# A windowed-attention block, rebuilt on full tiles: two score groups per transpose, values on both partition halves, key blocks made on ScalarE, three row buffers

## The chip, the cores and the metric

One core of a Trainium2 chip runs the whole program. The metric is device time in microseconds (us) of one execution. Three engines matter here: TensorE (PE in the profile; the loading of its stationary operand is shown apart, as PEld), VectorE (DVE) and ScalarE (ACT). GpSimd (POOL) and SyncE (SP) issue transfers and do small work. Each engine takes its instructions strictly in the order of its own queue; that order was fixed when the program was built, by a scheduler that interleaves everything the program contains.

## The reference, cut to what matters

Sixteen images of 56 x 56 positions and 128 channels go through four layers, each with its own group normalisation and a residual. Only the first layer, windowed attention, is touched by the change.

```python
def _L0_conv_ref(x, w_qkv, pos_emb, w_out, b_out):   # x: (16, 56, 56, 128)
    x = jnp.roll(x, (-DISP, -DISP), axis=(1, 2))      # DISP = 3
    q, k, v = jnp.split(x @ w_qkv, 3, axis=-1)
    q, k, v = (to_windows(q), to_windows(k), to_windows(v))  # 8 x 8 windows of 7 x 7, 4 heads of 32
    dots = jnp.einsum('bhwid,bhwjd->bhwij', q, k) * scale
    dots = dots + bias[None, None, None] + MASK[None, None]
    attn = jax.nn.softmax(dots, axis=-1)
    out = jnp.einsum('bhwij,bhwjd->bhwid', attn, v)
...
    return jnp.roll(out @ w_out + b_out, (DISP, DISP), axis=(1, 2))
...
x = x + _L0_conv_ref(_gn(x), ...)   # windowed attention
x = x + _L1_conv_ref(_gn(x), ...)   # triangle product
x = x + _L2_conv_ref(_gn(x), ...)   # Fourier attention
x = x + _L3_conv_ref(_gn(x), ...)   # bilinear
```

## The kernel before

Everything is fp32. An image lies in on-chip memory as `xt`, 128 channels on the partitions and 3136 positions along them. Images run in two lanes: even images in lane 0, odd ones in lane 1, each with its own working area (`arena`), its own two one-bank PSUM buffers (`psb`) and its own two-bank PSUM buffer (`psd`). Every image passes the four blocks in turn; the two lanes run beside each other, so the program is eight pairs of images, and within a pair both lanes are in the same block most of the time, lane A (the first to start) a little ahead of lane B.

The attention block (`_window_attention`, `run` from line 526) takes an image in eight rows of eight windows. A window has 49 positions, a row 392. For each row, in the order of the code:

- lines 544 to 546 gather the normalised row into `xw` (DVE does the part of seven windows, POOL the wrapped eighth); `xw` and all that follows lie in one of two halves of the arena, chosen by the row's parity;
- lines 547 to 549: queries on PE (408 columns), copied with a scale to `qt` by ACT;
- lines 550 to 559: keys on PE, then eight small copies (32 partitions x 196), four on DVE (line 559) and four on ACT (line 557), that place each head's 32 channels of the keys into `kblks`, two block tiles that are zero elsewhere (cleared once, line 530). With them one matmul scores all four heads of a window: the other heads' channels meet zeros. There is one such pair of tiles for all rows;
- lines 560 to 565: values, eight matmuls in two PSUM buffers of 49 partitions x 512, each copied to `vt` by ACT;
- lines 568 to 585: scores, two banks of four windows; even windows on partitions 0 to 63, odd ones on 64 to 127; DVE adds the bias on the way to `st`, 784 wide, in 16 groups (four pairs of windows x four heads) of 49;
- lines 586 to 594: the softmax over those 16 groups, five DVE instructions and one exponential on ACT (line 591);
- lines 596 to 603: 16 transposes of 128 x 49, four to a PSUM buffer; each of the four 49 x 512 results is copied to `atn`, two by DVE and two by ACT;
- lines 604 to 615: 32 small matmuls (49 x 32 stationary, 49 columns) weigh the values; ACT copies the result to `ot`;
- lines 616 to 620: the output projection, which DVE adds into `xt` in three pieces (six in the last row).

A row asks for 12 `psb` buffers in turn, and its lane has two, so each third request waits until the first buffer has been read out. In fp32 a matmul is issued as two passes on PE; a transpose is one.

Of the kernel before, what the change touches and what calls it, by code (L numbers as in the profile page):

```python
# [37 lines left out]
AF = mybir.ActivationFunctionType  # L38
# [4 lines left out]
P = 128  # L43
# [8 lines left out]
WS, DISP, NW = 7, 3, 8  # L52
WIN = WS * WS
NH0 = 4
ROWC = NW * WIN
# [38 lines left out]
def _constants():  # L94

    c = {}
# [29 lines left out]
    c["heads"] = np.kron(np.eye(8), np.ones((16, 1)))  # L126

    w, j, l33 = np.arange(P), np.arange(T), np.arange(33)
# [15 lines left out]
    C, S = cs(range(T))  # L144
    both("dv", (C, -S), (S, C))
    C, S = cs([e[1] for e in ENT])
    both("dx", (C, -S), (S, C))
    C, S = cs([e[2] for e in ENT])
    both("dya", (C, -S), (S, C))
    both("dyb", (-S, -C), (C, -S))  # L150
    C, S = cs([e[2] for e in MIR])
    both("dmx", (C, -S), (S, C))
    C, S = cs([e[3] for e in MIR])
# [4 lines left out]
    C, S = (pad(z) for z in cs([_rho(r, 14) for r in range(28)]))  # L158
# [20 lines left out]
    a = 2 * np.pi * np.outer(j, j) / T  # L179
    C, S = np.cos(a), np.sin(a)  # L180
# [4 lines left out]
    a = 2 * np.pi * np.outer(np.arange(32), w) / P  # L185
# [304 lines left out]
def _window_attention(env):  # L490
    e = _Env(env)
# [34 lines left out]
    def run(b, xt):  # L526
        nm, rs = e.group_norm(xt, W("bout0"))
        ar = e.arena()
        half_arena = 5120
        nc.gpsimd.memset(ar[:, 2 * half_arena : 2 * half_arena + 1568], 0.0)  # L530
        kblks = [
            ar[:, o : o + 784].rearrange("p (w h j) -> p w h j", w=NW // 2, h=NH0)
            for o in (2 * half_arena, 2 * half_arena + 784)
        ]
        for k in range(2):
            nc.gpsimd.memset(ar[:, k * half_arena + ROWC : k * half_arena + 408], 0.0)
        for wi in range(NW):
            o = wi % 2 * half_arena
            xw, qt, vt, st, atn, ot = (
                ar[:, o + a : o + a + n]  # L540
                for a, n in ((0, 408), (408, 408), (816, 1024), (1840, 784), (2624, 2048), (4672, ROWC))
# [5 lines left out]
            p = e.psb()  # L547
            mm(p[:, :408], lhsT=W("wqkv")[:, 0:128], rhs=xw, start=True, stop=True)
            nc.scalar.mul(qt, p[:, :408], scale)
            p = e.psb()  # L550
            mm(p[:, :ROWC], lhsT=W("wqkv")[:, 128:256], rhs=row, start=True, stop=True)
            for k, kb in enumerate(kblks):
                for h in range(NH0):
                    s = slice(32 * h, 32 * h + 32)
                    src = p[s, 196 * k : 196 * k + 196].rearrange("p (w j) -> p w j", j=WIN)
                    if h % 2:
                        nc.scalar.copy(kb[s, :, h, :], src)
                    else:
                        nc.vector.tensor_copy(kb[s, :, h, :], src)
            for g in range(2):  # L560
                p = e.psb()
                for i in range(4):
                    w = 4 * g + i
                    mm(p[:WIN, i * P : (i + 1) * P], lhsT=row[:, w * WIN : (w + 1) * WIN], rhs=W("wqkv")[:, 256:384], start=True, stop=True)
                nc.scalar.copy(vt[:WIN, g * 512 : (g + 1) * 512], p[:WIN, :])

            var = 1 if wi == NW - 1 else 0
            for bank in range(2):
                sc = e.psb()
                for w in range(4 * bank, 4 * bank + 4):  # L570
                    col = (w // 2 % 2) * 196
                    half = (w % 2) * 64
                    mm(
                        sc[half : half + 64, col : col + 196],
                        lhsT=qt[:, w * WIN : w * WIN + 64],
                        rhs=kblks[bank][:, w % 4].rearrange("p h j -> p (h j)"),
                        start=True,
                        stop=True,
                    )
                tt(  # L580
                    st[:, bank * 392 : bank * 392 + 392].rearrange("p (a h j) -> p a h j", a=2, h=NH0),
                    sc[:, :392].rearrange("p (a h j) -> p a h j", a=2, h=NH0),
                    bc(bias[:, var, 2 * bank : 2 * bank + 2, :], 2, NH0),
                    ALU.add,
                )
            s3 = st.rearrange("p (a j) -> p a j", j=WIN)
# [4 lines left out]
            act(st, st, AF.Exp)  # L591
# [4 lines left out]
            for g in range(4):  # L596
                p = e.psb()
                for i in range(4):
                    nc.tensor.transpose(p[:WIN, i * P : (i + 1) * P], s3[:, 4 * g + i, :], C("ident"))
                if g % 2:  # L600
                    nc.scalar.copy(atn[:WIN, g * 512 : (g + 1) * 512], p[:WIN, :])
                else:
                    nc.vector.tensor_copy(atn[:WIN, g * 512 : (g + 1) * 512], p[:WIN, :])
            p = e.psb()
            for w in range(NW):
                for h in range(NH0):
                    c0 = (w // 2 * NH0 + h) * P + (w % 2) * 64
                    mm(
                        p[32 * h : 32 * h + 32, w * WIN : (w + 1) * WIN],
                        lhsT=vt[:WIN, w * P + 32 * h : w * P + 32 * h + 32],  # L610
                        rhs=atn[:WIN, c0 : c0 + WIN],
                        start=True,
                        stop=True,
                    )
            nc.scalar.copy(ot, p[:, :ROWC])
# [895 lines left out]
```

## Time and profile before

| what | value |
|---|---|
| median of 8 runs | 13180.7 us (13156.99 to 13234.26) |
| the profiled execution | 13178.56 us, of which the instructions' span is 13176.8 us |
| mean granted TensorE clock | 0.865 of full speed |
| instructions in the span | 201901 |
| first matmul of line 608 in each pair | at 83, 1710, 3307, 4965, 6594, 8222, 9892 and 11539 us |
| attention in the second pair | first gather at 1674 us, last addition into `xt` at 1917 us |

The profile is one execution taken by the hardware profiler. Busy time is counted by engine; matmuls are pipelined, so the end of each is modelled, and a busy PE is not PE at its peak. A line such as L608 is a line of the kernel's source. A count of matmuls counts passes, so 32 matmuls show as 64. PEclk is the share of TensorE's clock that was granted.

### The profile page before, as it was taken

The numbers are of one execution on the slowest core, as the hardware profiler recorded it, in microseconds if no ns is written. First come the engines' busy times: TensorE is split into PE (matmuls) and PEld (weight loads), VectorE is DVE, ScalarE is ACT, GpSimd is POOL, SyncE is SP. The second block draws the span as 40 slices with busy tenths as digits, with TensorE's granted clock in tenths as the row PEclk, the third lists the DMA queues.
The fourth block names the chain that finished last, engine by engine and source line by source line (L and its number), as shares of the span: only waits on it lengthen the run. The fifth ranks groups of instructions, "written<-read, shape, count | busy, mean of one in ns | idle before, by whom it ended". The sixth has DMA issues, their size and how long they took to land. (4 is left out here: it accounts for less than half of the span.)

```text
span 13176.8 us, 201901 instructions
## 1 busy us (share of the span) xinstructions
PE 10162.4 (77%) x82624; PEld 5597.4 (42%) x82624; DVE 9352.2 (71%) x12225; ACT 3777.2 (29%) x6598; POOL 2474.3 (19%) x3387
## 2 busy tenths in 40 slices
PE   7787688876878768787688876878768787687876
PEld 4444255432545325453254532545325453254532
DVE  7775777768676576875768757676576765767757
ACT  4223142231413314232141321413214132141321
POOL 0132101330012300123002230022300223002230
PEclk9887898988988889888898888988889888898887
DMA  1265913569045690346904478044690446904468
GB/s 35 58 183 182 333 40 87 154 212 336 8 99 142 222 325 9 109 132 237 313 5 122 119 260 294 1 124 117 235 314 6 112 129 237 313 6 112 129 240 304
DMA packets 1091754, 2105.90 MB, mean 160 GB/s; under 512 B 98320, under 2 KB 974096, under 8 KB 1089680
## 3 DMA queue, kind: packets, MB, share of 16 engines
q1 hardware_dynamic: 560000, 823.95, 18.9%
q0 software_dynamic: 165120, 629.61, 17.8%
q10 hardware_dynamic: 365712, 639.44, 13.3%
q8 instruction: 654, 10.72, 0.3%
q14 instruction: 268, 2.20, 0.1%
HBM read 1412.73 MB, written 667.03 MB: 158 GB/s over the span
## 5 line engine op out<-in xcount | busy, mean ns | idle before, releaser
L1426 DVE TENSOR_TENSOR arena<-arena 128x1792 f32<-128x1792 f32 x1344 | 2645.2, 2017 | 639.6 <-PE psb L371 313.3
L1213 DVE TENSOR_TENSOR arena<-arena 112x1344 f32<-112x1344 f32 x1024 | 1565.4, 1553 | 364.7 <-DMA arena<-table 347.6
L371 PE MATMUL psb<-arena,cst 128*32 128x448 f32 x9792 | 1526.7, 657 | 0.0
L1211 POOL DMA_DIRECT2D arena<-table x2048 | 1057.3, 518 | 1977.8 <-DMA arena<-table 491.4
L368 PE MATMUL psb<-arena,cst 128*32 128x448 f32 x1408 | 798.1, 654 | 805.7 <-DVE arena L1426 768.4
L371 PE MATMUL psb<-arena 128*64 128x448 f32 (+2 forms) x4864 | 1256.9, 534 | 0.0
L368 PE MATMUL psb<-arena 112*64 112x448 f32 (+1 forms) x1280 | 693.4, 627 | 361.7 <-DVE arena L1103 220.5
L416 POOL TENSOR_TENSOR arena<-arena,power 112x32 f32<-112x32 f32 x224 | 839.4, 3765 | 106.1 <-DVE arena L1357 101.1
L371 PE MATMUL psd<-arena 112*64 112x224 f32 (+1 forms) x3072 | 770.4, 476 | 0.0
L368 PE MATMUL psd<-arena 112*64 112x448 f32 x1024 | 568.9, 642 | 177.8 <-DVE arena L1213 161.7
L371 PEld LDWEIGHTS psb<-arena 112*64 112x64 f32 (+1 forms) x4864 | 451.9, 155 | 523.4 <-issue 516.1
L1411 ACT COPY arena<-psd 128x896 f32<-128x896 f32 x336 | 303.6, 905 | 1251.9 <-DVE arena L1426 682.1
L368 PEld LDWEIGHTS psb<-arena,cst 128*32 128x32 f32 x1408 | 122.5, 120 | 1243.7 <-DVE arena L1426 961.2
L1103 DVE TENSOR_TENSOR arena<-w,coef 128x1792 f32<-128x1792 f32 x256 | 507.8, 2018 | 111.5 <-PE psb L371 91.3
L371 PE MATMUL psd<-arena,wgt 128*32 128x448 f32 x2688 | 533.6, 625 | 39.9 <-DMA arena<-padded 39.3
L371 PEld LDWEIGHTS psb<-arena,cst 128*32 128x32 f32 x9792 | 363.0, 124 | 447.2 <-issue 427.7
L688 PE MATMUL psd<-wgt,arena 128*64 128x128 f32 x7168 | 489.5, 282 | 45.1 <-DVE arena L700 34.5
L368 PE MATMUL psd<-arena,wgt 128*32 128x448 f32 x896 | 452.5, 626 | 81.6 <-DMA arena<-padded 59.8
L688 PEld LDWEIGHTS psd<-wgt,arena 128*64 128x64 f32 x7168 | 422.0, 138 | 177.6 <-issue 126.6
L917 PE MATMUL psb<-cst,arena 128*128 128x64 f32 (+1 forms) x2688 | 431.0, 330 | 67.9 <-ACT arena L884 35.1
L1325 ACT COPY w<-psb 128x448 f32<-128x448 f32 x336 | 178.5, 531 | 1017.9 <-PE psb L371 646.0
L917 PEld LDWEIGHTS psb<-cst,arena 128*128 128x128 f32 x2688 | 419.4, 245 | 107.9 <-ACT arena L884 40.0
(302 smaller groups left out, 19327.7 us busy)
## 6 DMA issues: line engine op xcount, KB each, us to landing
arena<-table POOLq DMA_DIRECT2D x2048, 294.0 KB, 9.1
dy<-w ACTq DMA_DIRECT2D x336, 1792.0 KB
arena<-dy SPq DMA_DIRECT2D x1344, 448.0 KB
arena<-padded SPq DMA_DIRECT2D x896, 162.8 KB
w<-x SPq DMA_DIRECT2D x112, 224.0 KB
out<-w SPq DMA_DIRECT2D x112, 224.0 KB
padded<-w ACTq DMA_DIRECT2D x336, 62.0 KB
arena<-arena POOLq DMA_DIRECT2D x16, 784.0 KB, 9.0
```

Of the source, the lines that this page charges most:

```text
L368: done = mm(**first)
L371: mm(**kw)
L416: ptt(dst, src, w, ALU.pow)
L688: mm(p[half : half + 64, i // 4, i % 4 * P : (i % 4 + 1) * P], lhsT=xh[:, c0 : c0 + 64], rhs=W(w).rearrange("p (k c) -> p k c", c=64)[:, : ...
L917: mm(p[:, 2 * i * nl : 2 * (i + 1) * nl], lhsT=src[:, t * P : (t + 1) * P], rhs=fc, start=True, stop=True)
L1103: tt(t4, bc(ys[c][:, l0 : l0 + 4, :], 1, 8), bc(coef[:, c, h0 : h0 + 8, l0 : l0 + 4], 3, T), ALU.mult,)
L1211: nc.gpsimd.dma_start(out=t[hh * T : (hh + 1) * T, :], in_=bc(tflat[q, two, hh], 0, T))
L1213: tt(t4, bc(x3[:, :, s], 1, 2), t4, ALU.mult)
L1325: nc.scalar.copy(t[:, :CH], p[:, :CH])
L1411: nc.scalar.copy(z, p[:, :, :CH])
L1426: tt(t4, bc(rep, 2, 2), bc(z, 1, 2), ALU.mult)
```

## The change

Only the attention block and one constant differ. The gather, the bias, the softmax formula, the projection and the addition are as before; line numbers below in brackets are those of the changed file. No transfer is added or removed.

- Buffers: the row's area shrinks from 5120 to 3768 columns, there are three of them in turn (row index modulo 3), and the key block tile exists twice (row index modulo 2).
- Keys: they are projected first, queries second. ACT makes the block tile alone: four activations over all 128 partitions (128 x 392), one for each head, each multiplying by a column of a new constant `pick` that is one on the head's 32 channels and zero elsewhere (line 551). DVE's four copies and ACT's four are gone, and the clearing of 1568 columns at the start too.
- Values: each window's matmul takes 64 columns of `xw` instead of 49 and goes to partitions 0 to 63 or 64 to 127, so that eight matmuls fill one PSUM buffer of 128 x 512 (line 559) with one ACT copy (line 566).
- Scores: each 49-wide group gets a pitch of 64 in `st`, which is 1024 wide and whose pad columns are cleared once for each buffer; the groups are ordered so that two groups of 64 stand side by side. The softmax instructions (lines 591 to 596) have the same element counts as before, in 16 x 49.
- Transposes: eight of 128 x 128 (two groups each) into two PSUM buffers, one copied by DVE and one by ACT (lines 602 to 606).
- Weighing: 32 matmuls as before, half on partitions 0 to 63 and half on 64 to 127, into the two banks of a `psd` buffer (line 613); ACT copies 128 x 392 from both banks (line 620).
- A row now asks for eight `psb` buffers and one `psd` buffer.

```diff
--- before.py
+++ after.py
@@ -124,6 +124,7 @@
                 r[n, h, :, i, n, 8 * h + i] = 1.0
     c["red"] = r.transpose(2, 3, 0, 1, 4, 5).reshape(P, 4 * 32)
     c["heads"] = np.kron(np.eye(8), np.ones((16, 1)))
+    c["pick"] = np.kron(np.eye(NH0), np.ones((32, 1)))

     w, j, l33 = np.arange(P), np.arange(T), np.arange(33)
     ang = 2 * np.pi * np.outer(w, l33) / P
@@ -526,93 +527,100 @@
     def run(b, xt):
         nm, rs = e.group_norm(xt, W("bout0"))
         ar = e.arena()
-        half_arena = 5120
-        nc.gpsimd.memset(ar[:, 2 * half_arena : 2 * half_arena + 1568], 0.0)
-        kblks = [
-            ar[:, o : o + 784].rearrange("p (w h j) -> p w h j", w=NW // 2, h=NH0)
-            for o in (2 * half_arena, 2 * half_arena + 784)
-        ]
-        for k in range(2):
-            nc.gpsimd.memset(ar[:, k * half_arena + ROWC : k * half_arena + 408], 0.0)
+        span = 3768
+        for k in range(3):
+            o = k * span
+            nc.gpsimd.memset(ar[:, o + ROWC : o + 408], 0.0)
+            nc.gpsimd.memset(ar[:, o + 1328 : o + 2352].rearrange("p (g j) -> p g j", j=64)[:, :, WIN:], 0.0)
         for wi in range(NW):
-            o = wi % 2 * half_arena
+            o = wi % 3 * span
             xw, qt, vt, st, atn, ot = (
                 ar[:, o + a : o + a + n]
-                for a, n in ((0, 408), (408, 408), (816, 1024), (1840, 784), (2624, 2048), (4672, ROWC))
+                for a, n in ((0, 408), (408, 408), (816, 512), (1328, 1024), (2352, 1024), (3376, ROWC))
+            )
+            kb = ar[:, 3 * span + wi % 2 * 1568 : 3 * span + wi % 2 * 1568 + 1568].rearrange(
+                "p (w h j) -> p h w j", w=NW, h=NH0
             )
             row = xw[:, :ROWC]
             for piece in pieces(wi):
                 eng = nc.vector if piece[1] == 7 else nc.gpsimd
                 eng.tensor_scalar(windows(row, piece), image(xt, piece), nm, rs, ALU.add, ALU.mult)
             p = e.psb()
+            mm(p[:, :ROWC], lhsT=W("wqkv")[:, 128:256], rhs=row, start=True, stop=True)
+            for h in range(NH0):
+                act(kb[:, h], p[:, :ROWC].rearrange("p (w j) -> p w j", j=WIN), AF.Identity, scale=C("pick")[:, h : h + 1])
+            p = e.psb()
             mm(p[:, :408], lhsT=W("wqkv")[:, 0:128], rhs=xw, start=True, stop=True)
             nc.scalar.mul(qt, p[:, :408], scale)
             p = e.psb()
-            mm(p[:, :ROWC], lhsT=W("wqkv")[:, 128:256], rhs=row, start=True, stop=True)
-            for k, kb in enumerate(kblks):
-                for h in range(NH0):
-                    s = slice(32 * h, 32 * h + 32)
-                    src = p[s, 196 * k : 196 * k + 196].rearrange("p (w j) -> p w j", j=WIN)
-                    if h % 2:
-                        nc.scalar.copy(kb[s, :, h, :], src)
-                    else:
-                        nc.vector.tensor_copy(kb[s, :, h, :], src)
-            for g in range(2):
-                p = e.psb()
-                for i in range(4):
-                    w = 4 * g + i
-                    mm(p[:WIN, i * P : (i + 1) * P], lhsT=row[:, w * WIN : (w + 1) * WIN], rhs=W("wqkv")[:, 256:384], start=True, stop=True)
-                nc.scalar.copy(vt[:WIN, g * 512 : (g + 1) * 512], p[:WIN, :])
+            for slot in range(4):
+                for odd in range(2):
+                    w = slot // 2 * 4 + 2 * odd + slot % 2
+                    mm(
+                        p[64 * odd : 64 * odd + 64, slot * P : (slot + 1) * P],
+                        lhsT=xw[:, w * WIN : w * WIN + 64],
+                        rhs=W("wqkv")[:, 256:384],
+                        start=True,
+                        stop=True,
+                    )
+            nc.scalar.copy(vt, p)

             var = 1 if wi == NW - 1 else 0
+            s5 = st.rearrange("p (e h o j) -> p e o h j", e=2, h=NH0, o=2)[:, :, :, :, :WIN]
             for bank in range(2):
                 sc = e.psb()
                 for w in range(4 * bank, 4 * bank + 4):
                     col = (w // 2 % 2) * 196
                     half = (w % 2) * 64
                     mm(
-                        sc[half : half + 64, col : col + 196],
+                        sc[half : half + 64, col : col + 196].rearrange("p (h j) -> p h j", j=WIN),
                         lhsT=qt[:, w * WIN : w * WIN + 64],
-                        rhs=kblks[bank][:, w % 4].rearrange("p h j -> p (h j)"),
+                        rhs=kb[:, :, w],
                         start=True,
                         stop=True,
                     )
                 tt(
-                    st[:, bank * 392 : bank * 392 + 392].rearrange("p (a h j) -> p a h j", a=2, h=NH0),
+                    s5[:, bank],
                     sc[:, :392].rearrange("p (a h j) -> p a h j", a=2, h=NH0),
                     bc(bias[:, var, 2 * bank : 2 * bank + 2, :], 2, NH0),
                     ALU.add,
                 )
-            s3 = st.rearrange("p (a j) -> p a j", j=WIN)
+            s3 = st.rearrange("p (g j) -> p g j", j=64)[:, :, :WIN]
             r = e.sm()
             mx, su = r[:, 0:16], r[:, 16:32]
             nc.vector.tensor_reduce(mx, s3, AX.X, ALU.max)
             tt(s3, s3, bc(mx, 2, WIN), ALU.subtract)
-            act(st, st, AF.Exp)
+            act(s3, s3, AF.Exp)
             nc.vector.tensor_reduce(su, s3, AX.X, ALU.add)
             nc.vector.reciprocal(su, su)
             tt(s3, s3, bc(su, 2, WIN), ALU.mult)

-            for g in range(4):
+            for g in range(2):
                 p = e.psb()
-                for i in range(4):
-                    nc.tensor.transpose(p[:WIN, i * P : (i + 1) * P], s3[:, 4 * g + i, :], C("ident"))
+                for h in range(NH0):
+                    c0 = g * 512 + h * P
+                    nc.tensor.transpose(p[:, h * P : (h + 1) * P], st[:, c0 : c0 + P], C("ident"))
                 if g % 2:
-                    nc.scalar.copy(atn[:WIN, g * 512 : (g + 1) * 512], p[:WIN, :])
+                    nc.scalar.copy(atn[:, g * 512 : (g + 1) * 512], p)
                 else:
-                    nc.vector.tensor_copy(atn[:WIN, g * 512 : (g + 1) * 512], p[:WIN, :])
-            p = e.psb()
-            for w in range(NW):
+                    nc.vector.tensor_copy(atn[:, g * 512 : (g + 1) * 512], p)
+            p = e.psd()
+            for slot in range(4):
                 for h in range(NH0):
-                    c0 = (w // 2 * NH0 + h) * P + (w % 2) * 64
-                    mm(
-                        p[32 * h : 32 * h + 32, w * WIN : (w + 1) * WIN],
-                        lhsT=vt[:WIN, w * P + 32 * h : w * P + 32 * h + 32],
-                        rhs=atn[:WIN, c0 : c0 + WIN],
-                        start=True,
-                        stop=True,
-                    )
-            nc.scalar.copy(ot, p[:, :ROWC])
+                    for odd in range(2):
+                        c0 = slot // 2 * 512 + h * P + slot % 2 * 64
+                        s = slice(64 * odd, 64 * odd + 64)
+                        mm(
+                            p[32 * h : 32 * h + 32, odd, slot * WIN : (slot + 1) * WIN],
+                            lhsT=vt[s, slot * P + 32 * h : slot * P + 32 * h + 32],
+                            rhs=atn[s, c0 : c0 + WIN],
+                            start=True,
+                            stop=True,
+                        )
+            nc.scalar.copy(
+                ot.rearrange("p (e o n) -> p o e n", e=2, o=2),
+                p[:, :, :196].rearrange("p o (e n) -> p o e n", e=2),
+            )
             p = e.psb()
             mm(p[:, :ROWC], lhsT=W("wout0"), rhs=ot, start=True, stop=True)
             for piece in pieces(wi):
```

## The prediction

> **What bounds the kernel now.** I read the page first: busy shares, then the chain of waits. No engine is full over the whole span:
>
> ```profile
> PE 10162.4 (77%) x82624; PEld 5597.4 (42%) x82624; DVE 9352.2 (71%) x12225; ACT 3777.2 (29%) x6598; POOL 2474.3 (19%) x3387
> ```
>
> The chain reaches back only to 12,047 us and meets no attention row of an earlier pair, so it can't price the change. I therefore read the stage itself, by windows (columns: engine busy us, instruction counts in brackets, granted clock, DMA share, GB/s):
>
> ```profile
> 1755.00:1775.00 20.00, 16.79 (x227) 11.04 (x224) 16.72 (x33) 10.06 (x22) 1.64 (x4) 1.00 0.00 1
> 1775.00:1795.00 20.00, 16.79 (x227) 11.14 (x225) 16.62 (x33) 9.56 (x20) 1.38 (x4) 1.00 0.01 2
> ```
>
> PE and DVE (first and third) are both busy 84% at full clock, with no transfers: the two lanes interlock. The timeline shows the tail of one row and the repeat for the other lane's:
>
> ```profile
> 157.43 0.90 PE L608 MATMUL psb<-arena 49*32 49x49 f32 x64
> 158.40 0.48 ACT L615 COPY arena<-psb 128x392 f32<-128x392 f32 x1 [1.09 <-PE psb L608]
> 158.94 0.93 PE L617 MATMUL psb<-arena,wgt 128*128 128x392 f32 x2 [0.61 <-ACT arena L615]
> ...
> 168.09 0.90 PE L608 MATMUL psb<-arena 49*32 49x49 f32 x64
> ```
>
> A row leaves every 10.66 us (157.43 to 168.09). By the starts of line 617 in the second pair, lane A's first row ends at 1712.2, its second at 1735.3, then six periods of one row of each lane end with A's last at 1865.1 (129.8 us, 21.6 a period), and B's last two end at 1879.3 and 1915.0, beside A's triangle. The groups of exactly six rows (1745 to 1809 us) price a row; divide busy by six:
>
> ```profile
> L599 PE MATMUL psb<-cst,arena 128*49 128x128 f32 x96 | 12.9, 278 | 0.0
> L564 PE MATMUL psb<-wgt,arena 128*49 128x128 f32 x96 | 12.9, 277 | 4.0 <-ACT arena L565 4.0
> L559 DVE COPY arena<-psb 32x196 f32<-32x196 f32 x24 | 8.5, 353 | 2.7 <-ACT arena L557 2.3
> L603 DVE COPY arena<-psb 49x512 f32<-49x512 f32 x12 | 8.2, 682 | 0.8 <-PE psb L599 0.8
> L557 ACT COPY arena<-psb 32x196 f32<-32x196 f32 x24 | 7.6, 315 | 9.3 <-DVE arena L559 8.6
> L565 ACT COPY arena<-psb 49x512 f32<-49x512 f32 x12 | 6.9, 578 | 3.1 <-PE psb L564 2.2
> ```
>
> The key copies of lines 557 and 559 wait for each other (8.6 us in six rows).
>
> **The change part by part**, per row; 128 rows in all.
> - DVE loses four key copies, 4 x 0.353 = 1.41, and one of two transpose copies, 0.68: 2.09 of about 9.2 us. The 128x512 copy that stays I take at the same 0.68: these rows go by columns (49x512 0.68, 128x392 0.57). The pitch of 64 changes no element count, so the softmax rows stay at 0.97.
> - ACT loses 4 x 0.315, one value copy and one transpose copy (2 x 0.578): 2.42. It gains four 128x392 activations with a scale column. No row shows that form. Low bound: line 615's plain copy, 0.485. High bound: line 662's with two columns, 0.760 for 448 columns, less 56 columns at 0.83 ns = 0.713. Nearest is line 456, from PSUM with one column: two of 448 columns in 1.15, so 0.575, less 0.047 = 0.53. I take 0.53, 2.12 in all; bounds 1.94 to 2.85. ACT stays near 5.1 us, but 2.12 of it is now one block that nothing can pass.
> - PE: values from 2 x 1.07 to one run of 16 passes in pairs on the column halves, as line 573 already runs (16 passes of 196 columns in 1.55): at 128 columns about 1.05. Transposes from 16 to 8 with 128-column weights; line 917 has such weights at full clock, 28 passes in 3.31, so 0.115 each and 1.06 for eight with fill. High bound: line 917's weight load exposed, 8 x 0.192 = 1.54. Weighing: 64 passes in 0.90 now; between 0.55 (row halves side by side) and 0.90; I take 0.65, for part of it overlaps. PE loses 2.4 of 9.6 us.
> - POOL clears about 770 columns per image in six pieces instead of 1600 (line 530: 1.40 us for 1568): at most 1 us sooner, hidden behind the first gather. No transfer issue moves into or out of the block, and none stands behind a new wait: SP and POOL's table loads belong to later blocks.
> - The program has 128 activation table loads instead of 118; at 1.283 us each that is 12.8 us of an engine that is 29% busy: 0, at most 13 if none is covered.
> - The third row buffer and second key tile: I take 0. In the changed queues the next row's key projection still stands right behind the output projection on PE, and two `psb` buffers allow no more. Bounds: 0 to the 0.9 of that projection.
>
> **Where it lies.** The changed queues again give A two rows alone, six shared periods, then two of B beside A's triangle. But the lanes now run nearly abreast instead of half a period apart. Playing one common period (four of the six) by the queue order, from the first of A's key activations (changed line 551) as zero, with these durations and 0.06 a hand-over: A's key blocks to 2.1, A's queries to 2.6, then B's weighted values (620), queued behind them, to 3.1; PE then has B's projection and B's keys to 4.85, A's scores to 5.5 and 6.2. B's key blocks and queries 4.9 to 7.5, B's values on PE to 8.1 and ACT to 8.7, B's second score bank to 9.7, its bias 10.3. DVE then does in order six 0.97 operations, two reciprocals (0.23) and A's transpose copy (0.68), in all 6.96: to 17.3. Then PE: B's transposes 1.06, with A's projection (0.8) and next keys (0.95) queued behind: 19.9, and the next period starts. One period has both lanes' steps strictly paired: the same sum gives 21.0, DVE carrying both softmaxes to 16.9; a mixed one I put between, 20.5. Mean (4 x 19.9 + 21.0 + 20.5)/6 = 20.2.
>
> **The clock takes that back.** In these periods PE has nothing from 9.7 to 14.5 (A's softmax ends there), 4.8 us. What such a hole costs, the windows show where the fourth pair begins (PE busy first, clock third from the end):
>
> ```profile
> 4974.39:4977.80 3.41, 1.12 (x12) 0.71 (x8) 3.12 (x7) 0.00 (x0) 1.68 (x3) 1.00 0.00 0
> 4977.80:4981.21 3.41, 2.53 (x4) 1.18 (x4) 0.67 (x1) 0.77 (x2) 1.51 (x3) 0.50 0.00 0
> 4981.21:4984.63 3.42, 2.63 (x11) 1.73 (x11) 2.78 (x5) 1.70 (x4) 0.00 (x0) 0.50 0.00 0
> 4984.63:4988.04 3.41, 3.41 (x16) 2.69 (x14) 1.89 (x5) 1.21 (x3) 0.71 (x2) 0.50 0.00 0
> 4988.04:4991.45 3.41, 3.07 (x65) 2.33 (x68) 2.33 (x5) 1.16 (x2) 0.00 (x0) 1.00 0.00 0
> ```
>
> A window of 3.41 us with PE busy a third of it is followed by half clock, until a window is nearly full. Counted so over the trace, 276 of 277 full-clock windows under 0.4 are followed by half clock, and no half-clock window under 0.7 ends it. A hole of 4.8 us always leaves one under 0.4. At half clock line 564's eight passes take 1.94, not 1.07, line 548 1.73, not 0.85. On the path lie B's transposes (+0.9) and then A's projection and keys (+1.7 if all at half clock; I take +1.0, the clock returning in the middle, about 20 us): +1.9 a period, 22.0 on the mean. Shared periods: 48 x (22.0 - 21.6) = +19 us.
>
> **The rows alone.** A lone row is one chain: a second round of transposes and copy goes (1.07 + 0.68), the alternation of eight copies (about 3.4 with hand-overs) becomes 2.12 and the queries' 0.49, and weighing gives 0.25: 2.5 a row, 5 for A's two. B's two share both engines with the triangle, which are 2.1 and 2.4 lighter a row: I take 2, so 4. Eight pairs: -72. Bounds: 0, if the lanes wait for a transfer later anyway, and twice that.
>
> **Sum** against the profiled execution: 13178.6 + 19 - 72 = 13,126; the median of the runs shown is 2.1 above it, so 13,128. Everything behind attention is queued in another order too. Before, equal pairs take 1627, 1598, 1658, 1628, 1628, 1670 and 1648 us (starts of line 608): spread 24, so 68 us for eight, either way. The likeliest case's own range: 13,060 to 13,190.
>
> **The rivals.**
> - *The clock holds*: shared periods of 20.2: 48 x -1.4 = -67, and -72: 13,042. For: PE may get triangle or gather work into the hole; against: 276 of 277. On this the Trainium skill (TensorE: Matmul & The Clock Gate, What's actually happening) says the clock falls after an idle window of about 3.4 us; a 4.8 us hole holds a whole free-running window in 0.41 of cases, which by that rule is an estimate of +0.7 a period and 13,072. The trace disagrees: the window above fell with 1.12 us busy.
> - *The lanes interlock again*: DVE at 86% of 7.1 us gives 8.2 a row, 16.4 a period: 48 x -5.2 - 72, so 12,859. For: the shares before. Against: the queue order itself, with two score buffers a lane.
> - *Slower: half clock lasts into the next front.* Three windows as above; then B's projection and keys are slow too (+1.6), 23.6 a period: 48 x 2.0 = +96, and with lone rows worth half, -36: 13,241. It decides from 23.1 a period, where 48 x 1.5 eats the 72. For: such a window must be nearly full, and each hand-over to ACT empties it. Against: the paired order fills PE behind the hole. A key activation at its high bound (8 x 0.18 = 1.5 a period) ends at the same place.
> - *The lead is waited off later*: the Fourier and bilinear blocks run at 0.9 to 1.0 DMA share for hundreds of us (600 to 900, 1300 to 1650); a lane that comes 9 us sooner may wait there: 13,180.
>
> **How the numbers follow.** No change means within 0.2%, 26 us, which is what a measurement can tell here. Forecast 0.38 (faster 0.23, same 0.10, slower 0.05); clock holds 0.17; interlock 0.07; slower 0.28 (0.02 of it within 26); waited off 0.10 (same 0.06, slower 0.04 with the spread). Faster 0.47, same 0.18, slower 0.35. Range 12,930 to 13,270: it leaves out the interlock and the far end of the slow case.
>
> **What would show it.** Line 551 at 0.53; transposes in two groups of about 0.6; line 606 at 0.68; steps of line 625 in pairs, 22 us a period; granted clock 0.7 to 0.9 instead of 1.00 in the middle of attention; PE idle before line 602 for DVE. It is wrong if the clock stays 1.00 there, if a period is under 19, or if pairs differ by more outside attention than in it.

## The result and the profile after

The changed kernel takes 13,135.1 us (median of 24 runs, 13,071.5 to 13,199.2) where the kernel before takes 13,188.5 (64 runs, 13,119.2 to 13,260.5). The ratio is 0.9957, with a 95% interval of 0.9945 to 0.9969: 57 us, or 0.43%, faster. The forecast was 13,128. The two profiled executions lie closer together than that, 13,153.9 us of span after and 13,176.8 before, so sums over the two traces must explain 23 us, not 57.

The busy line of the page after:

```profile
PE 10014.7 (76%) x81600; PEld 5515.8 (42%) x81600; DVE 9075.4 (69%) x11585; ACT 3733.6 (28%) x6352; POOL 2455.6 (19%) x3435
```

DVE was relieved of 277 us of work and PE of 148. Only a fifth of DVE's saving reached the time. The windows of the same stretch of the second pair as before the change say why (columns as before: PE first, DVE third, granted clock third from the end):

```profile
1755.00:1775.00 20.00, 15.55 (x212) 10.27 (x212) 12.34 (x24) 7.42 (x14) 2.36 (x6) 0.74 0.00 1
1775.00:1795.00 20.00, 13.72 (x212) 9.15 (x214) 11.98 (x20) 9.07 (x18) 0.81 (x2) 0.83 0.01 2
```

Both engines were busy 84% at full clock before; now PE is busy 69 to 78% and DVE 60 to 62%, at a clock of 0.74 to 0.83. The timeline of one period shows where the clock goes (start, duration, then the idle time before and what ended it):

```profile
1752.74 2.02 ACT L551 ACTIVATE arena<-psb,cst 128x392 f32<-128x392 f32 x4 [1.62 <-PE psb L549]
...
1755.74 1.77 PE L575 MATMUL psb<-arena 128*64 128x196 f32 x16
...
1758.26 0.56 DVE L582 TENSOR_TENSOR arena<-psb,cst 128x392 f32<-128x392 f32 x1
...
1758.89 0.93 DVE L591 TENSOR_REDUCE sm<-arena 128x16 f32<-128x784 f32 x1
1759.74 0.97 DVE L596 TENSOR_TENSOR arena<-arena,sm 128x784 f32<-128x784 f32 x1
...
1760.76 1.97 PE L602 MATMUL psb<-cst,arena 128*128 128x128 f32 x8 [3.25 <-DVE arena L596]
...
1764.94 1.94 PE L602 MATMUL psb<-cst,arena 128*128 128x128 f32 x8 [0.95 <-DVE arena L596]
...
1766.68 1.51 PE L625 MATMUL psb<-arena,wgt 128*128 128x392 f32 x2
...
1773.36 0.93 PE L625 MATMUL psb<-arena,wgt 128*128 128x392 f32 x2
```

After the scores of both lanes (line 575) PE has nothing for 3.25 us, until DVE has finished one lane's softmax (line 596). What follows the hole runs slowly: eight transposes in 1.97 us, an output projection in 1.51. One row later the clock is back, and the next output projection takes 0.93. The two projections, 6.7 us apart, are the two lanes' rows, which leave in pairs.

The groups of the stretch from 1744.8 to 1811.1 us, three periods and so six rows, that answer to those shown of before (busy us and mean ns of one behind the bar):

```profile
L551 ACT ACTIVATE arena<-psb,cst 128x392 f32<-128x392 f32 x24 | 12.2, 591 | 10.5 <-PE psb L549 10.5
L602 PE MATMUL psb<-cst,arena 128*128 128x128 f32 x50 | 11.6, 404 | 13.0 <-DVE arena L596 13.0
...
L613 PE MATMUL psd<-arena 64*32 64x49 f32 x384 | 6.6, 251 | 0.7 <-ACT arena L604 0.5 <-DVE arena L606 0.2
L559 PE MATMUL psb<-wgt,arena 128*64 128x128 f32 x96 | 6.6, 279 | 2.7 <-ACT arena L551 2.6
...
L606 DVE COPY arena<-psb 128x512 f32<-128x512 f32 x7 | 4.8, 690 | 5.8 <-PE psb L602 5.8
```

Values fell from 12.9 us to 6.6. The transposes, half as many, still take 11.6 of 12.9, and the wait ahead of them is 13.0 us in the six rows: these are the two prices, the hole and the slow clock behind it.

Followed along the chain that paces a pair, the two executions differ like this (sums over eight pairs, us; A and B are the lanes, an output is the start of line 617 before and 625 after, and a pair ends with the last pass of line 1458 before and 1466 after, the transposes of B's last piece; the first stretch of the first pair begins with the program):

```
                                                   before    after   difference
end of a pair to A's first output of the next        125.0     96.5    -28.5
A's first output to its second                       188.0    183.9     -4.1
A's second output to its last (six periods)         1045.9   1026.5    -19.4
A's last output to B's last                          370.2    399.9    +29.7
B's last output to the end of the pair             11442.4  11441.9     -0.5
to the end of the last pair                        13171.5  13148.7    -22.8
```

From A's first output to B's last, attention is not shorter than before: 1,610.3 us against 1,604.1. All that the two traces differ by lies ahead of A's first output: it comes sooner after the end of the pair before, in six of the seven later pairs right beside that end.

### The profile page after: what moved, and what is told of

The parts are those of the page before. It is cut to its first block, busy times and chain, and to the rows that moved or that the text cites. A ratio compares the mean times of both kernels' runs of the same rounds, so it can differ in the third digit from the quotient of the medians.

```text
span 13153.9 us, 198953 instructions
## 1 busy us (share of the span) xinstructions
PE 10014.7 (76%) x81600; PEld 5515.8 (42%) x81600; DVE 9075.4 (69%) x11585; ACT 3733.6 (28%) x6352; POOL 2455.6 (19%) x3435
## 5 line engine op out<-in xcount | busy, mean ns | idle before, releaser
L372 PE MATMUL psb<-arena,cst 128*32 128x448 f32 x9792 | 1507.8, 650 | 0.0
L369 PE MATMUL psb<-arena,cst 128*32 128x448 f32 x1408 | 788.6, 647 | 770.8 <-DVE arena L1434 746.2
L372 PE MATMUL psb<-arena 112*64 112x224 f32 (+2 forms) x4864 | 1254.1, 530 | 0.0
```

The costliest lines, as they stand in the source:

```text
L369: done = mm(**first)
L372: mm(**kw)
```

## The experiments

Three theories. The first: a lack of work on PE ahead of the transposes halves the clock, and this eats most of what the engines were spared. The second: the clock is only a companion, and the order in which the two lanes' work is queued, with its hand-overs, sets the period. The third: attention does gain, and the later blocks, which wait for transfers, take it back. Eight kernels hold attention alone, and so run the two lanes in attention from end to end; three are whole, and one is the whole without attention. In attention alone the changed kernel's lanes settle into the paired order (both lanes' rows end shortly one after the other), and each period shows plainly. The times in the table are medians of two runs, which lie within 0.7% of each other in each kernel. The first two kernels, attn_fill and attn_keys ran beside a kernel before of 13,231.7 us, the other four beside one of 13,142.6, so that differences between the two sets below 1% mean nothing.

```
kernel           us      of attn_after   clock   steady period
attn_before    1665.0     1.014          0.95    21.3 (10.7 a row)
attn_after     1642.3     1              0.82    mostly 21.9 and 22.3 in turn
attn_fill      1551.9     0.945          0.95    19.4
attn_keys      1727.3     1.052          0.80    about 22 (19 to 24)
attn_pairfill  1552.9     0.946          0.95    20.1, some 21 to 21.5
attn_stag      1595.8     0.972          0.89    18.8 (9.4 a row)
attn_two       1601.5     0.975          0.85    18 to 22, by pair
attn_bkeys     1803.2     1.098          0.90    24 (20.9 in the first pair)
```

**attn_before and attn_after**: attention alone, in both kernels.

```diff
-def tile_blocks(ctx: ExitStack, tc: tile.TileContext, ins, out, at, stages=(0, 1, 2, 3)):
+def tile_blocks(ctx: ExitStack, tc: tile.TileContext, ins, out, at, stages=(0,)):
```

> The kernel before with the other three blocks left out: only loads, attention and stores of the 16 images. Baseline for the next three. In the shared rows the lanes stand half a period apart, as in the whole kernel: a row leaves every 10.7 us (21.3 a period of one row of each lane), with the granted clock at 1.00 there and no hole of TensorE over 1.5 us. Some 64 periods and the ends of each image: 1,500 to 1,800 us in all. All theories agree here.

> The changed kernel with the same three blocks left out. Theory 1 (the clock takes the saved work back): TensorE waits over 3 us for the two softmaxes ahead of the transposes, the next windows run at half clock, a period takes 21.5 to 22.5 us, and the whole is no more than 2% faster than attn_before. Theory 2 (what is saved was never on the path: the hand-over between ScalarE's key block, TensorE and VectorE sets the period): the same period, but a period that meets full clock all through takes as long as one at half clock. Theory 3 (attention itself gains what the engines lost, and the rest of the kernel gives it back): a period of 20 us or less, the whole over 5% faster than attn_before.

Alone, the change is worth 1.4%. The period of the changed kernel is about 22 us, longer than the 21.3 of the kernel before, and its clock is down; the third theory, with its 20 us, is out. From attn_after, two windows of about one period each:

```profile
1144.00:1167.00 23.00, 17.34 (x220) 11.10 (x220) 13.48 (x24) 9.71 (x18) 0.00 (x0) 0.78 0.01 2
1167.00:1189.00 22.00, 15.77 (x220) 10.07 (x220) 12.82 (x23) 9.58 (x18) 0.00 (x0) 0.84 0.01 1
```

**attn_fill**: work without use on PE in the hole.

```diff
             nc.vector.tensor_reduce(mx, s3, AX.X, ALU.max)
+            pd = e.psd()
+            first = mm(pd[:, 0, 0:16], lhsT=C("ident"), rhs=mx, start=True, stop=True)
+            with e.tc.issue_after(first.ins):
+                for i in range(2):
+                    mm(pd[:, i], lhsT=C("ident"), rhs=e.cst[:, 0:512], start=True, stop=True)
...
-            p = e.psd()
+            p = pd
```

> attn_after with filler on TensorE: after the maximum of each row's softmax, one 16-column and two 512-column matmuls into the row's two-bank buffer, which the weighing overwrites afterwards; nothing reads them. They lie in the hole ahead of the transposes, about 2.2 us a row, 4.4 of its 4.8 us. Theory 1: the clock stays at 1.00 in the rows, transposes take 0.63 a group and not 0.98, the next keys and queries 0.85 and not 1.73, and a period falls to 20 to 20.6 us, over 5% less than attn_after. Theory 2: no shorter than attn_after although the clock is up, or longer by the filler that sticks out. Theory 3: no difference beyond 1%.

It is 5.5% faster than attn_after, and the clock is up. But the period is 19.4, below what the first theory allowed, and the steps are 11.5 and 7.9 us, not 15.6 and 6.7: with the filler in it the scheduler put lane B half a period behind. Clock and order changed together, so this run alone decides nothing. The next one holds the order.

**attn_pairfill**: filler in lane A's rows only, and the paired order fixed by edges that order TensorE's queue without waiting for a result. `behind(later, first)` queues one marked instruction behind another; marks name the image, the row and the step: K keys, S scores, F filler, T transposes, O output projection.

```diff
             nc.vector.tensor_reduce(mx, s3, AX.X, ALU.max)
+            pd = e.psd()
+            if b % 2 == 0:
+                done = mm(pd[:, 0, 0:16], lhsT=C("ident"), rhs=mx, start=True, stop=True)
+                e.marks[b, wi, "F", 0] = done
+                with e.tc.issue_after(done.ins):
+                    for i in range(3):
+                        done = mm(pd[:, i % 2], lhsT=C("ident"), rhs=e.cst[:, 0:512], start=True, stop=True)
...
+        if b % 2:
+            for j in range(7):
+                behind((b - 1, j + 1, "T", 0, 0), (b, j, "S"))
+                behind((b - 1, j + 1, "F", 0), (b, j, "S"))
+                behind((b - 1, j + 1, "O"), (b, j, "T", 1, 3))
...
```

> attn_fill raised the clock but its queues also came out in another order (lane B half a period behind, as in the kernel before), so its gain has two possible causes. Here the filler (one 16-column and three 512-column matmuls, about 2.9 us) stands in lane A's rows alone, and six order-only edges a row hold TensorE's queue in the paired order of attn_after: both lanes' scores, filler, A's transposes and weighing, B's transposes. Only attention runs, as in attn_after. If the clock alone costs (theory 1): granted clock over 0.95 in the rows, period 20.2 (19.8 to 20.6), 1,530 to 1,590 us in all. If the paired order costs (theory 2): clock up as well, but a period of 21.5 or more and no more than 2% gained on attn_after's 1642.

The same order, with a full clock, takes 20.1 us in most periods (steps of 5.3 and 14.8) where attn_after takes 21.9 and 22.3 in turn: the first theory, which had 20.2. In all it is 5.4% faster than attn_after; each taken against the kernel before that ran beside it (0.1181 and 0.1242 of it), 4.9%. PE's timeline of one period, first of attn_pairfill, where lines 604 and 608 are the filler and 620 the transposes:

```profile
1233.84 1.76 PE L585 MATMUL psb<-arena 128*64 128x196 f32 x16
1235.54 0.40 PE L604 MATMUL psd<-sm,cst 128*128 128x16 f32 x2
1235.78 2.82 PE L608 MATMUL psd<-cst 128*128 128x512 f32 x6
1238.86 1.09 PE L620 MATMUL psb<-cst,arena 128*128 128x128 f32 x8 [0.26 <-DVE arena L614]
...
1243.04 1.06 PE L620 MATMUL psb<-cst,arena 128*128 128x128 f32 x8 [1.52 <-DVE arena L614]
1243.94 0.82 PE L647 MATMUL psb<-arena,wgt 128*128 128x392 f32 x2
1244.60 0.82 PE L559 MATMUL psb<-arena,wgt 128*128 128x392 f32 x2
```

and then of attn_after:

```profile
1145.47 1.97 PE L602 MATMUL psb<-cst,arena 128*128 128x128 f32 x8 [3.26 <-DVE arena L596]
...
1149.66 1.94 PE L602 MATMUL psb<-cst,arena 128*128 128x128 f32 x8 [0.96 <-DVE arena L596]
1151.39 1.51 PE L625 MATMUL psb<-arena,wgt 128*128 128x392 f32 x2
1152.70 1.51 PE L549 MATMUL psb<-arena,wgt 128*128 128x392 f32 x2
```

The wait for the softmax is as long, 3.26 us idle against 3.32 of filler (from 1235.54 to 1238.86) with 0.26 of waiting in it. What differs is what comes after: transposes 1.09 and 1.06 instead of 1.97 and 1.94, output projection and next keys 0.82 instead of 1.51. The first of these four savings is not on the path: the second transposes wait for DVE (line 596, and 614 with filler), and start 4.18 us after the first in attn_pairfill and 4.19 in attn_after. The other three, 0.88, 0.69 and 0.69, make 2.26 us, and the period is 2.2 shorter. In the periods between, the half clock comes 1.05 us after the first transposes of attn_after have begun, and these take 1.09; the second still start 4.18 behind them, and the period is 21.9. The windows of attn_pairfill show the clock at 1.00:

```profile
1229.00:1249.00 20.00, 16.47 (x230) 9.83 (x228) 13.50 (x25) 9.44 (x19) 1.56 (x5) 1.00 0.00 1
1249.00:1269.00 20.00, 16.47 (x230) 9.71 (x227) 13.55 (x25) 9.46 (x19) 2.14 (x6) 1.00 0.01 2
```

**attn_stag**: no filler, but lane B half a period behind.

```diff
+        if b % 2:
+            for j in range(6):
+                behind((b - 1, j + 2, "T", 0, 0), (b, j, "S"))
+                if j < 5:
+                    behind((b, j, "T", 0, 0), (b - 1, j + 3, "S"))
```

> attn_after without any filler, with two order-only edges a row on TensorE that put lane B half a period behind: A's transposes stand behind B's scores, B's transposes behind the scores of A's next row. No work is added or taken away. If the order is what costs (theory 2): TensorE works on one lane while VectorE has the other's softmax, no hole over 1.5 us, clock 1.00 without help, period 18.2 (as six rows of attn_after's second pair had by chance: 9.1 a row), 1,430 to 1,530 us. If only the clock costs (theory 1) and the holes fall as before: clock about 0.82, 1,600 us or more.

The steady rows do as the second theory said, 9.4 us each at full clock, but the whole misses its range by 66 us. The images' ends got worse: the rows that run without a partner take 15 to 27 us, and the mean clock is 0.89. So order matters beyond the clock: at full clock a period is 18.8 us here and 20.1 in attn_pairfill. But what it gains in the middle is paid at the ends.

**attn_keys and attn_bkeys**: one part of the change undone (the first diff, against attn_after), and the same part done alone (the second, against attn_before).

```diff
-            for h in range(NH0):
-                act(kb[:, h], p[:, :ROWC].rearrange("p (w j) -> p w j", j=WIN), AF.Identity, scale=C("pick")[:, h : h + 1])
+            for k in range(2):
+                for h in range(NH0):
...
+                    if h % 2:
+                        nc.scalar.copy(kb[s, h, 4 * k : 4 * k + 4], src)
+                    else:
+                        nc.vector.tensor_copy(kb[s, h, 4 * k : 4 * k + 4], src)
```

```diff
-            for k, kb in enumerate(kblks):
...
+            for h in range(NH0):
+                act(kball[:, h], p[:, :ROWC].rearrange("p (w j) -> p w j", j=WIN), AF.Identity, scale=C("pick")[:, h : h + 1])
```

> attn_after with the key blocks made as before: eight copies of 32 partitions by 196 columns, four on VectorE and four on ScalarE, into the two tiles, which are cleared once. VectorE gets back 4 x 0.353 = 1.41 us a row, ScalarE loses 2.03 and gets 4 x 0.315 = 1.26. Theory 1: VectorE's share is on the path of the period, so 2 x 1.41 = 2.8 us more a period, and the hole is no shorter: 8 to 15% slower than attn_after. Theory 2 (ScalarE's block of four activations holds up the queries and the other lane's weighted values): a period no longer, or up to 1 us shorter than in attn_after, since one lane's hand-overs pass between the copies. Theory 3: between, 3 to 8% slower.

> attn_before (values, transposes and weighing as before, attention only) with one part of the change: the key blocks made by ScalarE in four activations of 128x392. VectorE loses 1.41 us a row. Theory 2 (the order decides): the queues of this kernel still have lane B half a period behind, so the clock stays at 1.00 and a row falls from 10.67 to 9.3 to 10 us: 1,480 to 1,600 us, faster than attn_after with all the parts. Theory 1 (less VectorE work opens holes on TensorE whatever the order): the clock falls and the whole stays over 1,620.

The parts do not add up. Key blocks on ScalarE alone make attention 8.3% slower than attn_before; the other parts alone (attn_keys) 3.7% slower; both together 1.4% faster. Both expectations failed in their mechanism, though attn_keys's 5.2% lies in a range that was named. In attn_keys the period is no longer than in attn_after, about 22: the 5.2% that it loses lie at the ends of the images, where the lanes now come together, 54 to 58 us from the last output of one pair to the first of the next against 23 to 26 in attn_after's later pairs. In attn_bkeys the lanes stayed half a period apart only in the first pair: there a row leaves every 10.4 us instead of 10.7, where the second theory had 9.3 to 10, so the key blocks on ScalarE gained 0.2 us a row there. In the other pairs rows leave in steps of 14 to 17 and 7 to 11 us and the clock falls, which steady windows of it show beside one of attn_before:

```profile
720.00:740.00 20.00, 16.28 (x223) 10.39 (x221) 12.21 (x24) 11.11 (x21) 1.45 (x4) 1.00 0.01 2
740.00:760.00 20.00, 16.85 (x206) 11.60 (x207) 10.35 (x20) 8.07 (x16) 0.72 (x2) 0.83 0.00 1
```

```profile
740.00:760.00 20.00, 16.79 (x227) 11.09 (x224) 16.78 (x34) 9.61 (x20) 1.43 (x4) 1.00 0.01 2
```

DVE falls from 16.8 us to 10 to 12 of 20, and nothing is gained. How much of the 138 us is clock and how much the changed order was not separated.

**attn_two and full_two**: two row buffers instead of three.

```diff
-            o = wi % 3 * span
+            o = wi % 2 * span
```

> attn_after with two row buffers in turn, not three. All theories: the third buffer is worth nothing, since two psb buffers a lane hold the next row back: within 1% of attn_after's 1642. A rival: it lets the next gather and keys start early, then 1 to 4% slower.

> The whole changed kernel with two row buffers, not three; here TensorE's queue comes out in nearly the same order as in the changed kernel (in attention alone it had come out otherwise, and 2.5% faster). If the third buffer is worth nothing: within 0.3% of the changed kernel, 0.993 to 0.998 of the kernel before. If it helps: over 0.999. If it harms (an order by which A's rows run ahead into the half clock): under 0.992.

Alone, two buffers are 2.5% faster than three (1.9% when each is taken against the kernel before beside it); in the whole kernel they are slower, 0.9993 of the kernel before (0.9976 to 1.0009), where the changed kernel is at 0.9957. The lanes are arranged otherwise in both. In full_two, lane B's first output comes 33 to 137 us behind A's second in the last five pairs (5 to 22 with three buffers from the second pair on), and B's rows run beside A's triangle; nearly the same order, as the expectation has it, is seen in the first three pairs alone. So the buffer's own price stays open, and its effect on the order is larger.

**full_stag, full_pairfill**: the edges of attn_stag, and filler and edges of attn_pairfill, in the whole kernel. There A leads by two rows, so each edge of attn_pairfill ties A's row to B's two rows earlier.

> The whole changed kernel (all four blocks) with attn_stag's two order-only edges a row on TensorE in each pair's six shared periods: B's transposes behind the scores of A's next row, A's behind B's scores. Theory 1 (what attention saves arrives at the end): in attn_stag a shared period took 18.8 us at full clock against 22.3 in the paired order, so 48 x -3.5 = -168 us, less up to 70 for worse ends of an image (two rows alone cost attn_stag some 8 us a pair): 12,970 to 13,080 us, 0.984 to 0.992 of the kernel before, clock 1.00 in the shared rows. Theory 3 (the Fourier and bilinear transfers take back what attention gains): attention shorter by as much, but over 0.993 of the kernel before.

> The whole changed kernel with attn_pairfill's filler in lane A's rows and its order-only edges, which keep TensorE's queue in the order of the changed kernel. In attention alone this took 5.4% off (period 20.1 and not 22.3). Theory 1 (the half clock is the price, and it arrives at the end): 48 x -2.2 = -106 us, up to 30 of it lost to filler in the rows that run alone: 0.987 to 0.991 of the kernel before. Theory 3: attention shorter by as much, but within 0.3% of the changed kernel, 0.993 to 0.999 of the kernel before.

full_pairfill takes 13,102.1 us, 0.9928 of the kernel before (0.9905 to 0.9951): the lowest of all, though its interval, from four runs, still touches that of the changed kernel (0.9945 to 0.9969). Its shared rows run near full clock, 0.94 to 0.98 in the second, third, fifth and eighth pairs, where the changed kernel has 0.81, and in these two windows of the third pair at 1.00:

```profile
3374.00:3394.00 20.00, 16.59 (x231) 9.99 (x219) 13.11 (x25) 9.81 (x18) 2.68 (x6) 1.00 0.01 2
3394.00:3414.00 20.00, 16.20 (x227) 9.44 (x225) 13.05 (x23) 9.56 (x18) 0.81 (x2) 1.00 0.01 2
```

It gains about 0.29% over the changed kernel, 38 us, where the expectation had 76 to 106, and this is not clear of the noise. In its trace, the end of a pair to B's last output of the next takes 1,662.7 us in eight pairs, where the changed kernel's has 1,706.8: 44 us less, but 41.6 of them lie ahead of A's first output. The expectation's failed step is to have given the changed kernel 22.3 us in all 48 periods. In the seven pairs behind the first, the mean from A's second output to its last is 21.2 us there, and 21.0 in full_pairfill: periods of 20.1 it has, but one pair waits 34 us at its first shared row, and B's first step takes about 25 in most pairs. What a full clock in the shared rows is worth in the whole kernel thus stays open.

full_stag takes 13,194.2 us, 1.000 of the kernel before (0.9983 to 1.0017): the period is 18.8, as in attn_stag, and nothing arrives. Most of what the shared rows gain is lost in attention itself. From the end of a pair to B's last output of the next it has 1,697.8 us in eight pairs, against 1,706.8 in the changed kernel and 1,729.1 before: of the 168 us that the shared periods were to gain over the changed kernel, 9 are left. In four pairs A's third output came 30 to 58 us after its second, since the edges hold A back until B has come; and B, now a good half period further behind, has its last rows 69 to 76 us after A's last, beside the triangle, where it was 50. Behind B's last output its trace has 11,493.0 us, 51 more than before; pairs of one kernel differ there by up to 65 us, so one trace can't tell whether the order costs this. The edges put B one of A's rows further back than the kernel before does; a version with one row less was not tried.

**full_noattn**: attention left out of the whole.

```diff
-def tile_blocks(ctx: ExitStack, tc: tile.TileContext, ins, out, at, stages=(0, 1, 2, 3)):
+def tile_blocks(ctx: ExitStack, tc: tile.TileContext, ins, out, at, stages=(1, 2, 3)):
```

> The kernel with attention left out: loads, triangle, Fourier and bilinear blocks and stores of the 16 images, which are the same in both kernels. It tells what attention is worth in the whole. Theory 1 (attention's time arrives 1:1): 13,190 less the 1,604 us that the lanes' outputs span in attention in the kernel before, and less some 40 for the first gathers: 11,500 to 11,600 us. Theory 3 (part of attention lies beside work that bounds the pair anyway, so a us saved there arrives in part): above 11,700; each 160 us above 11,590 is a tenth of attention that is hidden.

It takes 11,546.3 us beside 13,170.7 of the kernel before: attention costs 1,624 us in the whole (1,594 to 1,674 by the interval of the ratio), and 1,604 from A's first output to B's last. As a whole it arrives about one to one, so the later blocks do not hide it, which speaks against the third theory a second time. This says what attention is worth as a whole; that each us saved at its edge arrives is not shown by it.

## Why the prediction was right, and where it was not

The time was right to 7 us, in part by luck. Its main claim held: a hole of PE ahead of the transposes, half clock behind it, and a paired period no shorter than before. But two terms of the sum were off by 38 and 62 us, one each way, so that they cancelled in part; and the two traces differ by 23 us where the medians differ by 53, so that 30 us of the gain are explained by no trace.

- *Durations.* Four key activations take 2.03 us (predicted 2.12), values 1.09 (1.05), DVE's transpose copy 0.69 (0.68), eight transposes at full clock 1.09 (1.06). The weighing was mis-sized: two halves of 0.41 us at full clock, and 0.36 between them while ACT copies the second group (1.2 from start to end, not 0.65).
- *The period at full clock*, 20.2 by the queue order (whose last step adds up to 20.1 and not 19.9): 20.1 in most periods of attn_pairfill. *The period with the clock's fall*, 22.0: 21.9 and 22.3 in turn in attn_after, and about 22 in the paired periods of the whole kernel. The clock's price, predicted +1.9, is 1.8 and 2.2, and the path is the predicted one: the second lane's transposes, then the projection and the keys behind them. The hole was put at 4.8 us. In the changed kernel's trace 50 waits of over 2.5 us stand ahead of line 602, 14 of them 3.25 us long and the others 4.3 to 8.5, and half clock sets in during each of the 50 or within 1.9 us of its end. The reason given, that such a hole always leaves a window under 0.4, does not cover the 14.
- *Shared periods, +19 us.* They came out at -19.4, a mean of 21.4 against one of 21.8 before (the forecast took 21.6 from the second pair). The step that failed is that all six periods were given the half clock's 22.0: several periods have other steps, 18.4 to 21, where the lanes lie further apart.
- *Lone rows, -72 us.* A's two were priced at -40 (the savings listed for a row add up to 2.8 us and not 2.5, which would be -45): its first row, with the end of B's pair before it, gained 28.5, and its second 4.1, so -33. B's last two, priced at -32, went to +29.7. That term had the wrong sign, and its failed step is to have priced B's rows by their work alone: B's first output is further behind A's second than before (93.7 us in eight pairs instead of 66.2), and these 27.5 us are nearly the whole of the loss. The lone rows together gave -3.
- *Third buffer: 0.* Not settled; what it does to the order is worth some 0.4% of the whole.
- *The rivals.* "The clock holds" was priced at 13,042, 139 us below the kernel before; with filler to hold it, full_pairfill comes to 0.9928, 95 us below. "Half clock lasts into the next front": after the hole it lasts over the transposes, one projection and the next keys (1.51 each, or 1.52 and 1.15 in the periods between), and the next projection is at 0.93, so it ends a little later than the forecast put it, and well short of the rival. "The lead is waited off later": B's chain, which ends the kernel, has 0.5 us less after attention than before, and full_noattn speaks against it too. "Interlock": it can be had, at 18.8 us a period and not 16.4, but not for nothing.
- *The Trainium skill* (TensorE: Matmul & The Clock Gate, What's actually happening) ties the fall of the clock to an idle window. By that rule the forecast's own terms, 0.41 of +1.9, make an estimate of +0.8 a period and 13,079, not +0.7 and 13,072. In the changed kernel's trace all 330 full-clock windows of 3.41 us with PE busy below 0.4 were followed by half clock, and of the 1971 with more than 0.6, 41 were (windows as the clock's own records mark them; counted so, the kernel before has 298 of 300 below 0.4, where the forecast has 276 of 277). Most of the 330 are not idle: in 244 PE was busy for over a tenth. The measurement decides, as it did in the forecast.

## What to carry to other kernels

Taking work off two engines that take turns can open a hole on the third, TensorE, whose clock then falls (here 3.25 to 8.5 us, and half clock with each); look for the stretches of the new queue order in which TensorE is busy under 0.4 of a 3.4 us window, and price at half speed those matmuls behind them that lie on the path. Where such a hole can't be closed, 3 us of matmuls without use in it can pay (5.4% in attention alone; in the whole kernel about 0.3%, which is not clear of the noise). And read the effect of one part only in the order that the build makes of it: parts that each made attention slower made it faster together, and the order moved with every edit.

## What the chip showed that was not expected

The clock does not go by the amount of matmul work in a period. In attn_stag's steady rows PE is busy 15 of 20 us and the clock is at 1.00 without any filler:

```profile
720.00:740.00 20.00, 15.05 (x242) 9.52 (x236) 13.77 (x25) 10.82 (x20) 1.15 (x3) 1.00 0.01 2
```

The changed kernel's windows at the top have 13.7 to 15.6 busy us of 20, at 0.74 to 0.83. Idle is a quarter there and 22 to 31% here; in the one it comes in pieces of at most 1.5 us, in the other a piece of 3.25 is among them. Such a piece is not the only way to a fall: in attn_bkeys 52 of the 60 falls of the clock come at the end of windows that no idle stretch of PE over 3 us touches. And matmuls that nobody reads, 3.2 us a period, made a period 2.2 us shorter.
